# Writing the order of an image's work as one list, with norm sums on VectorE and pruning sums on ScalarE

## The chip, the cores and the metric

The kernel runs on one core of one Trainium2 chip. The metric is the device time of one execution in microseconds (us). Most executions of a kernel agree within 0.3% (41 of the kernel before, taken with e1_psv: 2678.42 to 2688.64 us, median 2684.96). Each ratio below is between fast runs of a kernel and of the kernel before that ran on the same chip in alternation. Where two edited kernels are held against each other, they often ran on different chips; then each goes through its own ratio to the kernel before.

## The reference, cut to what matters

Eight images of 512 channels by 32 x 32, all in fp32. Two residual layers follow each other. Layer 0 is heavy on matmuls, layer 1 on elementwise work.

```python
def reference(x, ...):
    x = x + layer0(group_norm(x))     # 32 groups
    x = x + layer1(group_norm(x))
    return x

def layer0(x):                        # C = 256
    t = silu(bn(conv1x1(x)))          # cv1
    ys = [t[:, :C], t[:, C:]]
    for i in range(2):
        z = silu(bn(conv3x3(ys[-1])))
        z = attention(z)              # 4 heads of 64, 1024 positions; q, k, v from a 1x1 conv
        z = silu(bn(conv1x1(z)))
        ys.append(ys[-1] + z)
    return silu(bn(conv1x1(concat(ys))))    # cv2, the last convolution

def layer1(x):
    h = relu(bn(depthwise3x3(x) + b))
    h = where(max|h| of the channel < 4.0, 0, h)      # pruning
    h = relu(bn(conv1x1(h) + b))
    return where(max|h| of the channel < 1e-3, 0, h)  # pruning
```

## The kernel before

TensorE (PE) does the matmuls of one image after another, and layer 1 of image b-1 is done beside layer 0 of image b: its depthwise taps run on VectorE (DVE), while PE is in the convolutions and attention of the next image. Each engine is given its instructions in the order in which the program emits them. A helper makes sure that no scheduler changes that:

```python
class InOrder:                 # every engine but GpSimd is wrapped in it
    ...
    if self.last is not None:
        self.tc.add_manual_dep(made.ins, self.last, how, reason="in_order")
```

So the text of the program is the queue of each engine. Background work lies in lists of pieces, and the main flow takes a few off a list here and there with `pump(list, n)`. The parts that the argument needs:

```python
def reaches(t, i):             # pruning test: a pass on ScalarE and a 0.15 us test on VectorE
    keep = small.tile([P, 1], F32, tag="keep3", name="keep3")
    nc.scalar.activation(
        work_tile("over"), t, AF.Relu, bias=below[:, i : i + 1], accum_out=keep
    )
    nc.vector.tensor_scalar(keep, keep, 0.0, None, ALU.is_gt)
    return keep
...
    def prune(c):              # layer 1, after the depthwise taps of chunk c
        if c < 2:
            keep = reaches(ht[c], 0)
        else:
            keep = small.tile([P, 1], F32, tag="keep", name="keep")
            nc.vector.tensor_reduce(keep, ht[c], AX.X, ALU.max)
            nc.vector.tensor_scalar(keep, keep, 4.0, None, ALU.is_ge)
        nc.gpsimd.tensor_scalar(ht[c], ht[c], keep, 1.0, ALU.mult, ALU.mult)
    ...
    for c in range(KC):
        mine = [lambda c=c, t=t: tap(c, t) for t in range(9) if t != 4]
        if c:                  # two taps of a chunk carry the end of the chunk before
            mine[2] = lambda c=c, t=mine[2]: (t(), relu(c - 1))
            mine[5] = lambda c=c, t=mine[5]: (t(), prune(c - 1))
        taps += mine
    taps += [lambda: relu(KC - 1), lambda: prune(KC - 1)]
...
def qkv(l, bg, counts):
    ...
    pump(bg, counts.pop(0))
    for m, ps in enumerate(products((2, 3), b == 0)):      # PE: ps_qk, two banks
        ...                                                # VectorE empties a bank into kr
        nc.vector.tensor_tensor(kk, phases(flat(ps)), col..., ALU.add)
        nc.gpsimd.tensor_tensor(kk, kk, row..., ALU.add)
        pump(bg, counts.pop(0))
    for g in range(2):
        ps = ps_big.tile([P, 4, C2], F32, tag="big", name="ps_v")   # needs one of the two banks
        ...                                                # PE: ps_v
        nc.scalar.copy(vt[:, 4 * g : 4 * g + 4, :], ps)
        pump(bg, counts.pop(0))
    for m in range(2):
        (ps,) = products((m,))
        nc.scalar.copy(qy[:, m, :], flat(ps))
        pump(bg, counts.pop(0))
...
    qkv(0, taps, (3, 0, 3, 2, 2, 2, 0))                    # images 1 to 7
```

In the first attention a softmax denominator is used in `scale` (`if s in (29, 30): scale(0, s - 29)`). In the last convolution the pieces of the next image's group norm (`pump(stats)`) stand between products. Layer 1 takes its norm sums with two ScalarE passes per chunk.

## Time and profile before

| | |
|---|---|
| time | 2683.93 us median of 3 runs (2683.41 to 2686.81) |
| PE | 2605.2 us busy; its steady steps sum to 2538 us |
| VectorE, ScalarE | 1999.7 us, 1252.0 us busy |
| lateness of PE by image 0 ... 7 | 30.5, 5.4, 12.1, 12.1, 12.1, 12.1, 14.9, 30.3 us |

"Lateness" is what PE's matmuls start later than the steady step of their kind would have them start, summed over an image; the prediction gives the steps. A name such as ps_v stands for the matmuls that write the tile of that name: ps_qk and ps_v make an attention's queries, keys and values, ps_s its scores, ps_av the sums of values weighted with them, ps_dn the sums of the softmax denominators; pm and pv are the two small ones of a group norm (means, then deviations, from the VectorE tiles mv and d), and ps_pw is layer 1's 1x1 convolution. Read the busy shares and slices first to find the engine that sets the end, then who that engine waits for, then the timeline around the longest wait. The prediction shows these. Two more lines carry the argument here. The chain of work that ended last, by engine:

```profile
PE 76%; DVE 16%; ACT 4%; issue 2%; DMA 1%; POOL 0%; SPq 0%; ACTq 0%; POOLq 0%; DVEq 0%
```

And VectorE's pruning test in the view of groups (count, busy us, mean ns, then the idle time ahead of it and what ended it):

```profile
L43 DVE TENSOR_SCALAR keep<-keep 128x1 f32<-128x1 f32 x64 | 9.8, 153 | 37.9 <-ACT over L43 36.4
```

64 instructions of 0.15 us, and VectorE stood 37.9 us in front of them. VectorE is not the engine that sets the end, so this may cost nothing; it costs something where PE needs VectorE next.

### The profile page before, as it was taken

The numbers are of one execution on the slowest core, as the hardware profiler recorded it, in microseconds if no ns is written. First come the engines' busy times: TensorE is split into PE (matmuls) and PEld (weight loads), VectorE is DVE, ScalarE is ACT, GpSimd is POOL, SyncE is SP. The second block draws the span as 40 slices with busy tenths as digits, with TensorE's granted clock in tenths as the row PEclk, the third lists the DMA queues.
The fourth block names the chain that finished last, engine by engine and source line by source line (L and its number), as shares of the span: only waits on it lengthen the run. The fifth ranks groups of instructions, "written<-read, shape, count | busy, mean of one in ns | idle before, by whom it ended". The sixth has DMA issues, their size and how long they took to land.

```text
span 2685.7 us, 36237 instructions
## 1 busy us (share of the span) xinstructions
PE 2605.2 (97%) x14862; PEld 1364.0 (51%) x14862; DVE 1999.7 (74%) x2708; ACT 1252.0 (47%) x1609; POOL 162.7 (6%) x99
## 2 busy tenths in 40 slices
PE   7999999999999999999999999999999999999996
PEld 5364464644636446364554545455464544645442
DVE  8786588776886768867788677886777866788556
ACT  3535545255453554535544345544445344453544
POOL 1000010000100001000010000100001000010000
PEclk9999999999999999999999999999999999999998
DMA  8443231411304013040231312222131221303100
GB/s 331 153 149 124 66 135 32 145 31 65 137 25 153 16 63 138 24 153 17 79 121 40 138 32 96 89 71 107 32 133 52 83 95 51 118 16 98 56 16 33
DMA packets 74238, 235.99 MB, mean 88 GB/s; under 512 B 6096, under 2 KB 34000, under 8 KB 59984
## 3 DMA queue, kind: packets, MB, share of 16 engines
q1 hardware_dynamic: 70512, 230.19, 24.4%
q10 hardware_dynamic: 3552, 3.41, 0.4%
q8 instruction: 118, 1.93, 0.3%
q14 instruction: 56, 0.46, 0.1%
HBM read 183.77 MB, written 33.03 MB: 81 GB/s over the span
## 4 chain that ended last, share of the span: by engine, by line
PE 76%; DVE 16%; ACT 4%; issue 2%; DMA 1%; POOL 0%; SPq 0%; ACTq 0%; POOLq 0%; DVEq 0%
PE ps_s L43 13%; PE ps_av L43 13%; PE ps_cv L43 9%; PE ps_pw L43 7%; PE ps_c L43 7%; PE ps_cv2q L43 7%; PE ps_qk L43 6%; PE ps_v L43 4%; DVE sum L43 4%; PE ps_m L43 4%; PE ps_y L43 3%; DVE mid L43 2%; DVE ht L43 2%; DVE y L43 1%; PE ps_dn L43 1%
## 5 line engine op out<-in xcount | busy, mean ns | idle before, releaser
L43 ACT ACTIVATE e<-ps_s 128x1024 f32<-128x1024 f32 x512 | 522.6, 1023 | 273.7 <-PE ps_s L43 263.9
L43 PE MATMUL ps_s<-qy,kr 64*64 64x512 f32 x4096 | 583.6, 593 | 3.8 <-ACT e L43 1.6
L43 PE MATMUL ps_av<-e,vt 64*64 64x512 f32 x4096 | 584.0, 591 | 1.6 <-ACT part L43 1.6
L43 DVE TENSOR_TENSOR sum<-sum,e 128x1024 f32<-128x1024 f32 x384 | 470.1, 1224 | 69.8 <-ACT e L43 62.4
L43 DVE SCALAR_TENSOR_TENSOR ht<-xn,v_sb,ht 128x961 f32<-128x961 f32 (+1 forms) x256 | 340.7, 1334 | 10.2 <-ACT ht L43 6.0
L43 PEld LDWEIGHTS ps_av<-e,vt 64*64 64x64 f32 x4096 | 206.1, 133 | 254.2 <-issue 198.3
L43 PEld LDWEIGHTS ps_s<-qy,kr 64*64 64x64 f32 x4096 | 191.1, 133 | 270.6 <-issue 164.8
L43 PE MATMUL ps_pw<-ht,wpw_sb 128*128 128x512 f32 x512 | 229.5, 604 | 7.6 <-DVE wpw_sb L43 7.6
L43 PE MATMUL ps_qk<-z,wring 128*128 128x512 f32 x512 | 228.9, 598 | 3.6 <-ACT z L43 3.6
L43 DVE TENSOR_TENSOR sum<-e 128x1024 f32<-128x1024 f32 x64 | 78.3, 1223 | 186.8 <-ACT e L43 186.2
L43 PEld LDWEIGHTS ps_pw<-ht,wpw_sb 128*128 128x128 f32 x512 | 97.4, 193 | 131.4 <-issue 121.4
L43 PEld LDWEIGHTS ps_qk<-z,wring 128*128 128x128 f32 x512 | 97.0, 191 | 122.5 <-issue 108.9
L43 PE MATMUL ps_v<-wring,z 128*128 128x256 f32 x512 | 118.3, 391 | 19.6 <-DVE kr L43 19.6
L43 ACT COPY c<-ps_c 128x256 f32<-128x256 f32 x96 | 35.4, 369 | 210.3 <-PE ps_c L43 204.1
L43 DVE RECIPROCAL r<-ps_dn 128x128 f32<-128x128 f32 x128 | 114.8, 928 | 11.8 <-ACT r L43 11.8
L43 PEld LDWEIGHTS ps_c<-kr,wring 128*128 128x128 f32 x1024 | 116.9, 192 | 10.3 <-issue 6.2
L43 PEld LDWEIGHTS ps_v<-wring,z 128*128 128x128 f32 x512 | 99.7, 196 | 43.7 <-DVE kr L43 26.2
L43 PE MATMUL ps_c<-kr,wring 128*128 128x128 f32 x1024 | 117.3, 275 | 2.2 <-ACT kr L43 2.2
L43 PE MATMUL ps_c<-vt,wring 128*128 128x128 f32 x1024 | 117.2, 275 | 0.7 <-ACT c L43 0.7
L43 PE MATMUL ps_c<-qy,wring 128*128 128x128 f32 x1024 | 117.6, 276 | 0.2 <-issue 0.2
L43 PE MATMUL ps_cv<-pt,w_sb 128*128 128x512 f32 x256 | 117.4, 609 | 0.0
L43 PEld LDWEIGHTS ps_c<-qy,wring 128*128 128x128 f32 x1024 | 116.1, 192 | 0.4 <-issue 0.3
(176 smaller groups left out, 3169.1 us busy)
## 6 DMA issues: line engine op xcount, KB each, us to landing
wring<-u SPq DMA_DIRECT2D x96, 1024.0 KB, 4.8
pt<-in_x SPq DMA_DIRECT2D x32, 512.0 KB, 6.5
rw<-r SPq DMA_DIRECT2D x64, 256.0 KB, 3.3
xt<-in_x SPq DMA_DIRECT2D x32, 512.0 KB, 5.9
out<-xt SPq DMA_DIRECT2D x32, 512.0 KB, 2.9
wring<-in_wqkv SPq DMA_DIRECT2D x16, 768.0 KB, 4.2
wring<-s SPq DMA_DIRECT2D x12, 1024.0 KB, 5.6
wring<-s SPq DMA_DIRECT2D x12, 768.0 KB, 5.2
```

The source lines that it names most:

```text
L43: made = method(*args, **kwargs)
```

## The change

The intent is to fix the order of all engines' queues in one written list per image. All work is cut into named pieces; a word takes the next piece of that name, `t*2` takes two. What was glued together (a tap with a relu, a pruning pass with its test, a matmul of the norm with what follows it) becomes separate words. A middle image has 449 words for 527 pieces and a closing list of 101 words. Two kinds of sum change engine as well: layer 1's norm sums go from ScalarE passes to VectorE's bn_stats, and all of layer 1's input pruning goes to ScalarE passes.

```diff
+HEAD = """
+    c*2 b im id bm c ca iv t ip t l t*2 lr ib b c bm ca b t y t*2 d y bm d ya d ya d*5 y P Rc ya
+    R d*2 P Rc R d P d Rc R B P Rc R B P B Rc R E P Rc B Ez R E Ez y k*3 ya X k ka dp kp t lp ka
+    t*2 kp t*2 v*2 va t l t v*2 va t*2 lr lp q*4 qa s qa s e*2 t p s t e w t p s e w p l s*2 w
     ... (ten more lines; and FIRST, TAIL and LAST alike)
-    def pump(bg, n=1):
+    def go(plan, without=()):
+        for word in plan.split():
+            name, _, n = word.partition("*")
+            if name in without:
+                continue
+            for _ in range(int(n or 1)):
+                todo[name].pop(0)()
...
-    def reaches(t, i):
+    def excess(t, i):
         keep = small.tile([P, 1], F32, tag="keep3", name="keep3")
         nc.scalar.activation(
             work_tile("over"), t, AF.Relu, bias=below[:, i : i + 1], accum_out=keep
         )
+        return keep
+
+    def positive(keep):
         nc.vector.tensor_scalar(keep, keep, 0.0, None, ALU.is_gt)
-        return keep
...
-        gn = [group_norm_scalar(xt, normed, chunks) for chunks in groups]
+        for chunks in groups:
+            group_norm("i im id iv ip ib b", xt, normed, chunks)
...
+        def reach(c):
+            keep[c] = excess(ht[c], 0)
+
         def prune(c):
-            if c < 2:
-                keep = reaches(ht[c], 0)
             ... (and the VectorE reduction for chunks 2 and 3)
+            positive(keep[c])
...
+            add("t", *[lambda c=c, t=t: tap(c, t) for t in range(9) if t != 4])
+            add("l", lambda c=c: relu(c))
+            add("lr", lambda c=c: reach(c))
+            add("lp", lambda c=c: prune(c))
```

The words used below: `k` a ps_qk product, `ka` its emptying into kr by VectorE, `kp` GpSimd's part of it, `v` and `va` a ps_v product and its copy, `t` a tap, `l` a relu, `lr` a pruning pass on ScalarE, `lp` its test on VectorE, `X` the load of ScalarE's exponential table (1.28 us in image 6 of the changed kernel, from the end of one activation at 1975.92 to 0.01 us before the next), `e` an exponential, `w` its addition to the sums, `h` the scaling of a half of the values, `nc` a check of the denominators, `x0` a residual half and `i` a half chunk's norm sums.

## The prediction

> **What bounds the kernel now.** I read the page's busy shares first, then the slices, then who waited for whom on PE, then the timeline around the longest of those waits.
>
> ```profile
> span 2685.7 us, 36237 instructions
> PE 2605.2 (97%) x14862; PEld 1364.0 (51%) x14862; DVE 1999.7 (74%) x2708; ACT 1252.0 (47%) x1609; POOL 162.7 (6%) x99
> PE   7999999999999999999999999999999999999996
> PEclk9999999999999999999999999999999999999998
> ```
>
> PE is busy in every slice but the first and last, so PE sets the end and only PE's lost time can be won. Busy time hides part of that loss, because the drawn ends of matmuls overlap the next start. So I work from start times in the timeline: at full clock, records of 512 columns start 0.4295 us apart, of 256 columns 0.2155, of 128 columns 0.1117, and four 64x64 records [...] share one step of 0.4295. With the counts of the groups view: 2720 x 0.4295 + 512 x 0.2155 + 3072 x 0.1117 + 8192/4 x 0.4295 + 256/4 x 0.4295 + about 10 for the small ones of the norms = 1168 + 110 + 343 + 880 + 27 + 10 = 2538 us. The change leaves all of these matmuls. The span has 2686 - 2538 = 148 us more: 7.8 before PE's first record, 10.2 after its last start, some 129 between. Adding up the late starts by image (each begins with its first ps_cv record) gives about 30 us for image 0, 5 for image 1, 12 for each of 2 to 5, 15 for 6 and 30 for 7.
>
> PE's waits, from the waits view of PE alone:
>
> ```profile
> PE ps_v L43 <- DVE kr L43: 19.6, 8, 3.1
> PE pv L43 <- DVE d L43: 8.7, 8, 1.2
> PE ps_dn L43 <- DVE sum L43: 8.2, 6, 1.4
> PE pm L43 <- DVE mv L43: 7.8, 1, 7.8
> PE ps_pw L43 <- DVE wpw_sb L43: 7.6, 3, 3.7
> PE pm L43 <- ACT ht L43: 4.3, 2, 2.3
> ```
>
> Columns: who waited for whom, us in total, times, longest. Nearly all is PE waiting for a late VectorE. Measured by start times the same places cost an image of the middle 3.25 us (ps_v), 2.0 (ps_dn) and 1.33 (pv); the rest of its 12 us is many steps of 0.1 to 0.5 us. Image 1 has neither of the first two, and shows what a good order reaches: 5.4.
>
> The timeline of image 6 at the ps_v wait:
>
> ```profile
> 2019.13 0.15 DVE L43 TENSOR_SCALAR keep<-keep 128x1 f32<-128x1 f32 x1 [3.47 <-ACT over L43]
> 2019.20 3.23 DVE L43 SCALAR_TENSOR_TENSOR ht<-xn,v_sb,ht 128x992 f32<-128x992 f32 x2
> ...
> 2022.36 3.82 DVE L43 TENSOR_TENSOR kr<-ps_qk,v_sb 128x1024 f32<-128x1024 f32 x2
> 2024.35 5.92 PE L43 MATMUL ps_v<-wring,z 128*128 128x256 f32 x13 [3.08 <-DVE kr L43]
> ```
>
> VectorE stood 3.47 us before a 0.15 us pruning test that waits for ScalarE, then did depthwise taps, and only then emptied the ps_qk bank that ps_v needs. Nothing here is short of throughput; the order is wrong.
>
> [...] the taps stood ready behind that test for 3.47 us. So the written order is the order done. [...]
>
> ```profile
> 2008.00:2020.60 12.60, 12.60 (x48) 6.85 (x47) 7.46 (x17) 6.02 (x8) 1.15 (x1) 1.00 0.88 336
> 2020.60:2023.30 2.70, 0.67 (x2) 0.00 (x0) 2.70 (x2) 0.83 (x1) 0.82 (x1) 1.00 0.01 6
> 2023.30:2030.10 6.80, 5.75 (x14) 4.59 (x15) 6.76 (x4) 0.41 (x1) 4.80 (x2) 0.50 0.00 0
> ```
>
> Columns: window, length, busy us (records) of PE, PEld, DVE, ACT, POOL, then the granted clock. It is 0.50 after the gap; PE starts there are 2.9 us later than the steady step. The late starts inside such half-clock stretches sum to about 17 us in the kernel, some 14 of them after waits in its course. [...]
>
> **The change part by part.** Rows for the sizes (groups, one row per shape):
>
> ```profile
> L43 ACT ACTIVATE ht<-xt 128x1024 f32<-128x1024 f32 x32 | 33.5, 1048 | 15.4 <-DVE xt L43 15.4
> L43 ACT ACTIVATE ht<-xt,gm 128x1024 f32<-128x1024 f32 x32 | 36.4, 1139 | 20.4 <-DVE gm L43 20.4
> L43 DVE BATCH_NORM_STATS2 st<-pt 128x6 f32<-128x512 f32 x64 | 40.9, 681 | 4.7 <-DMA pt<-in_x 4.7
> L43 DVE TENSOR_REDUCE keep<-ht 128x1 f32<-128x1024 f32 x14 | 17.0, 1212 | 0.0
> L43 ACT ACTIVATE over<-ht,below 128x1024 f32<-128x1024 f32 x18 | 20.5, 1141 | 0.1
> ```
>
> 1. Norm sums of layer 1 to VectorE. The built programs show 64 ScalarE passes gone (33.5 + 36.4 and 2 x 6.0 for their accumulator reads = 82 us) and 64 bn_stats (0.681), 32 aggregates (0.209) and 54 small operations (0.16) more on VectorE: 43.6 + 6.7 + 8.6 = 59 us.
> 2. The layer-1 input pruning to ScalarE: 14 reductions gone (17.0 us of VectorE), 14 passes with read (1.141 + 0.188) more: 18.6 us on ScalarE. Sum: VectorE 2000 + 42 = 2042 us, ScalarE 1252 - 63 = 1189. Neither is the bound, so this alone moves no time; what counts is where it falls. The added sums lie in the closing stage of an image (last convolution), the removed ones in the first attention, where VectorE is fullest.
> 3. The order. Matmul counts stay the same. For a middle image I walked the lists with the durations above:
>  - ps_v: the first bank is now emptied after the second of four ps_qk pieces (1.72 us each) with no tap ahead; 1.98 us end within the 3.44 of the two pieces left. The second follows one tap and ends some 2 us into the 3.44 us of the first ps_v group. The 3.25 us go; so do the half-clock stretches after it (2.9 in image 6, 1.6 in image 7).
>  - ps_dn: three value pieces (0.86 each) stand between the last exponential and the sums. The exponential and its addition (1.02 + 1.22) fit into 2.58. The 2.0 go.
>  - pv: a whole product (3.44 us) now stands between the two norm matmuls, for 0.65 us of VectorE. The 1.33 go.
>  - Two taps move from the first part to the closing stage; with two reductions less, VectorE has 2 x 1.33 + 2 x 1.21 = 5.1 us less up to the end of the first attention: about 109 us (its durations less 5%, as starts overlap) for PE's 126.
>  - Closing stage: VectorE has about 43 us for PE's 56, in spite of the sums.
> So images 2 to 6 fall to about 4.3 us of lateness: 4 x 7.7 + 10.5 = 41; image 1 gives 1. Image 7 has the first part too: 3.25 + 2.0 + 1.6 = 7, and its norm chain at the end, where PE waited 4.3 us for ScalarE's passes, perhaps 2 more; its end stays bound by taps. Image 0's start is bound by the weight transforms on VectorE in both; I give 5. Sum: 41 + 1 + 9 + 5 = 56. I add back 1 for small new waits: 2684 - 55 = **2629**; the written lists look searched for image 0 and the end too, for which I take another 4: **2625 us**.
>
> **The rivals.**
> - *VectorE becomes the bound in the first part.* Between the last product of an image and the first transformed convolution it has about 19 us of taps, norm and residual work, then 5.4 of input transform, against 24.1 us of PE; one late tap stalls PE. For it: VectorE is busy 85% in 670 to 737 us already. Against: drawn durations exceed its real steps by about 0.08 us. At 2 us an image: 2640.
> - *A new wait takes the old one's place.* PE is in order too, and norm matmuls now wait for VectorE where ScalarE served; all pruning passes also take a work buffer. If half of the gain returns: 2655.
> - *The lists remove nearly all lateness, also in images 0 and 7.* With 4 us in each middle image, 18 in the outer two, and shorter throttled stretches: 2610.
>
> **Range and chances.** Eight times in ten between 2608 and 2648; the low end is the third rival, the high end the first plus a part of the second. A gain over 2% needs less than 2630: 0.60. Within 2%: 0.39. Slower by over 2%: 0.01, as PE's work does not change and slack is large.
>
> **What would show it.** Right: PE's wait of ps_v for kr falls from 19.6 to under 3 us, ps_dn for sum and pv for d nearly vanish, no half clock in mid-kernel, VectorE about 2040 us busy, ScalarE about 1190, images of some 320 us instead of 327.5. Wrong: PE waiting for convolution inputs (ps_c for kr), for z or for e, or images 0 and 7 changing by more than 15 us. One thing I saw in the built order: in images 1 to 6 the sums of a chunk are read before its last residual half is added; that would change values a little, not the time.

## The result, and the profile after

| | before | after |
|---|---|---|
| time, median (range) of 4 runs each | 2684.28 us (2683.41 to 2686.81) | 2624.26 us (2622.55 to 2626.34) |
| PE, VectorE, ScalarE busy | 2605.2, 1999.7, 1252.0 | 2578.2, 2020.8, 1179.0 |
| lateness by image 0 ... 7 | 30.5, 5.4, 12.1 x 4, 14.9, 30.3 | 24.5, 4.0, 4.3, 4.0, 4.0, 4.0, 4.0, 14.9 |
| its sum | 129 | 64 |

The ratio is 0.9775 (95% interval 0.9758 to 0.9792): faster by 2.25%. Ratios here are the mean time of one kernel's fast runs over that of the other's of the same rounds, so they are not quite the ratio of the medians.

The page of the changed kernel, to be held against the lines at the head of the prediction:

```profile
span 2621.1 us, 36162 instructions
PE 2578.2 (98%) x14862; PEld 1328.7 (51%) x14862; DVE 2020.8 (77%) x2844; ACT 1179.0 (45%) x1509; POOL 169.9 (6%) x99
```

PE has the same 14862 matmuls, and they take 27 us less "busy" time. Some 10 us of that, at most, is half clock (the clock is at 0.50 for 31 us before and for 10 after); where the rest comes from was not looked for. Who PE waited for, of the changed kernel (us in total, times, longest):

```profile
PE pm L105 <- DVE mv L105: 9.5, 2, 7.8
PE ps_pw L105 <- DVE wpw_sb L105: 5.4, 2, 4.7
PE pv L105 <- DVE d L105: 4.2, 5, 0.8
...
PE ps_v L105 <- DVE kr L105: 1.1, 2, 0.8
```

ps_v for kr fell from 19.6 to 1.1 us, ps_dn for sum from 8.2 to nothing that is listed. What is left at the head of the list stands in image 0 and image 7. The chain of work that ended last, by engine:

```profile
PE 90%; DVE 4%; ACT 3%; issue 1%; DMA 0%; POOL 0%; SPq 0%; POOLq 0%; DVEq 0%; ACTq 0%
```

And the pruning test in the view of groups:

```profile
L105 DVE TENSOR_SCALAR keep<-keep 128x1 f32<-128x1 f32 x64 | 9.6, 150 | 11.0 <-ACT over L105 10.0
```

VectorE's share of the chain went from 16% to 4%, and its standing in front of the 64 tests from 37.9 to 11.0 us. The timeline of image 6 at the place where the prediction showed the ps_v wait (weight loads left out):

```profile
1974.55 7.03 PE L105 MATMUL ps_qk<-z,wring 128*128 128x512 f32 x16
...
1978.18 1.98 DVE L105 TENSOR_TENSOR kr<-ps_qk,v_sb 128x1024 f32<-128x1024 f32 x1 [4.21 <-PE ps_qk L105]
...
1981.20 0.14 DVE L105 TENSOR_SCALAR keep<-keep 128x1 f32<-128x1 f32 x1
1981.41 5.78 PE L105 MATMUL ps_v<-wring,z 128*128 128x256 f32 x26
```

VectorE now stands idle for 4.21 us, waiting for PE, and PE goes from ps_qk to ps_v without a gap. The test comes without a wait: its pass ran on ScalarE long before. Two things are different from before at this place, then: no taps ahead of kr, and no wait at the test. Which of the two matters is what the experiments had to find.

### The profile page after: what moved, and what is told of

Its sections match the earlier page's. It is cut to its first block, busy times and chain, and to the rows that moved or that the text cites. A ratio compares the mean times of both kernels' runs of the same rounds, so it can differ in the third digit from the quotient of the medians.

```text
span 2621.1 us, 36162 instructions
## 1 busy us (share of the span) xinstructions
PE 2578.2 (98%) x14862; PEld 1328.7 (51%) x14862; DVE 2020.8 (77%) x2844; ACT 1179.0 (45%) x1509; POOL 169.9 (6%) x99
## 4 chain that ended last, share of the span: by engine, by line
PE 90%; DVE 4%; ACT 3%; issue 1%; DMA 0%; POOL 0%; SPq 0%; POOLq 0%; DVEq 0%; ACTq 0%
PE ps_av L105 16%; PE ps_s L105 15%; PE ps_c L105 12%; PE ps_cv L105 10%; PE ps_qk L105 8%; PE ps_cv2q L105 8%; PE ps_pw L105 8%; PE ps_v L105 4%; PE ps_m L105 4%; PE ps_y L105 4%; PE ps_dn L105 1%; DVE ht L105 1%; ACT qy L105 1%; ACT e L105 0%; ACT over L105 0%
## 5 line engine op out<-in xcount | busy, mean ns | idle before, releaser
L105 ACT ACTIVATE e<-ps_s 128x1024 f32<-128x1024 f32 x512 | 510.6, 1023 | 272.7 <-PE ps_s L105 262.2
L105 PE MATMUL ps_s<-qy,kr 64*64 64x512 f32 x4096 | 537.9, 592 | 4.4 <-ACT e L105 3.1
L105 PE MATMUL ps_av<-e,vt 64*64 64x512 f32 x4096 | 536.3, 590 | 1.4 <-ACT part L105 0.7
L105 DVE SCALAR_TENSOR_TENSOR ht<-xn,v_sb,ht 128x961 f32<-128x961 f32 (+1 forms) x256 | 326.7, 1283 | 8.5 <-ACT ht L105 5.0
L105 PEld LDWEIGHTS ps_av<-e,vt 64*64 64x64 f32 x4096 | 183.9, 133 | 271.2 <-issue 237.5
L105 PEld LDWEIGHTS ps_s<-qy,kr 64*64 64x64 f32 x4096 | 173.6, 132 | 281.5 <-issue 169.8
L824 POOL TENSOR_TENSOR kr<-kr,v_sb 128x1024 f32<-128x1024 f32 x32 | 75.8, 2370 | 993.6 <-DVE kr L105 993.6
L105 PEld LDWEIGHTS ps_c<-vt,wring 128*128 128x128 f32 x1024 | 115.6, 192 | 3.8 <-issue 3.8
```

The costliest lines, as they stand in the source:

```text
L105: made = method(*args, **kwargs)
L824: nc.gpsimd.tensor_tensor(kk, kk, row.to_broadcast(full), ALU.add)
```

## The experiments

Theory at the outset: PE lost its time to the order of the queues, and each of the three waits of a middle image (ps_v 3.25, ps_dn 2.0, pv 1.33 us) goes when the order at its place is mended. Rival 1: the moves of sums between engines bring the gain. Rival 2: an order mended in one place only moves the wait. Every kernel here gave a correct result and every profile was of the fast state.

### One place at a time, in the kernel before

e1_psv, no tap ahead of the emptying of the banks:

```diff
-            qkv(0, taps, (3, 0, 3, 2, 2, 2, 0))
+            qkv(0, taps, (0, 0, 6, 2, 2, 2, 0))
```

> The kernel before with one edit: the three taps (and the pruning test among them) that stand ahead of emptying the ps_qk banks in the first attention block now stand behind it. Theory (only the order of VectorE's queue is at fault): PE's wait of ps_v for kr, 3.25 us in each of images 2 to 7, goes, and with it the half-clock stretches after two of them (4.5 us): 2684 - 24 = about 2660. Rival (VectorE is too full there, so a delayed tap makes something else late): no more than 8 us gained, 2676 or more, with PE waiting instead for sums or exponentials in the first attention.

Measured: 2692.23 us, ratio 1.0027 (1.0020 to 1.0035). A miss. The waits of PE in this kernel no longer have the ps_v wait near the top; another stands there:

```profile
PE ps_qk L43 <- ACT vt L43: 20.1, 6, 3.4
```

The timeline of image 3 (counted from 0) shows how:

```profile
1048.63 1.24 ACT L43 ACTIVATE ht<-ht,bi,sc 128x1024 f32<-128x1024 f32 x1 [10.24 <-DVE ht L43]
...
1050.82 3.70 PE L43 MATMUL ps_qk<-z,wring 128*128 128x512 f32 x8 [3.35 <-ACT vt L43]
```

Six pieces now stand together behind the banks. One is a tap with a relu glued to it. On ScalarE that relu stands ahead of the two copies that free ps_v's banks, and it waits 10.24 us for a tap that VectorE reaches late. PE waits 3.35 us where it had waited 3.1. In this stretch a mended queue of VectorE is paid for in ScalarE's queue. Part of the rest is half clock: it now follows this wait in images 2, 4, 5, 6 and 7, where the kernel before has it in images 6 and 7 only (mean granted clock of the profiled runs 0.993 and 0.994). Image 3, without it, is 327.8 us long against 327.5.

e2_dn moves `scale(0, .)` from steps 29 and 30 of the attention to 32 and 33, so that its two VectorE operations no longer stand ahead of the last sums:

> The kernel before with one edit: the two scalings of z in the attention stand behind the last addition of exponentials instead of ahead of it. Theory (order): the wait of ps_dn for the last addition, 2.0 us in each of images 2 to 7, goes: 2684 - 12 = about 2672. Rival (VectorE too full, or the wait only moves to the next user of z): under 4 us gained, 2680 or more, with PE waiting at ps_m or ps_pw.

Measured: 2686.30 us, ratio 1.0008 (1.0000 to 1.0017). The ps_dn wait went from 8.2 to 3.3 us in the trace, about 0.8 us an image; a 1.21 us pruning reduction still stands among the last sums. A miss, yet most middle images became longer, not shorter (328.4 us for 327.5), though no wait in them grew. What grew is half clock. The windows view of 3.4 us behind the ps_v wait of image 3, which no edit touched, in the kernel before and in e2_dn (columns as in the prediction, the third number from the end is the granted clock):

```profile
1041.80:1045.20 3.40, 3.40 (x16) 3.01 (x17) 3.37 (x3) 0.00 (x0) 3.40 (x2) 1.00 0.02 5
1042.30:1045.70 3.40, 3.40 (x9) 2.75 (x10) 3.37 (x3) 0.00 (x0) 3.40 (x2) 0.53 0.02 5
```

The wait is 3.25 us in both. In e2_dn half clock follows it in each of images 2 to 7, and costs 1.6 us or more a time (0.47 x 3.4 in this window); all its 12 runs have a mean granted clock of 0.991 or 0.992, the kernel before 0.994 to 0.997. So the edit won about 0.8 us an image, and the clock took it back.

e123 takes e1, e2 and one more edit, which puts a product between the two matmuls of the next image's norm:

```diff
-            pump(stats)
             product(0, "s3")
+            pump(stats)
```

> The kernel before with three edits of order: the two of the other runs, and one more product between the two norm matmuls of the closing stage (1.33 us in each of images 1 to 6 lost there). No engine gets other work. Theory (order): the gains add up, 24 + 12 + 8 = 44 us: about 2640, that is some three quarters of what the whole change gave (60). Rival (engine balance is needed too): they do not add up, 2655 or more.

Measured: 2678.25 us, ratio 0.9971 (0.9958 to 0.9983). The pv wait fell from 8.7 to 1.7 us, ps_dn for sum is at 3.3, and ps_qk for vt stays at 20.1. A gain of 7 us, where the three waits sum to over 36; the time is on the rival's side (2655 or more). Here too half clock follows the vt wait in images 2, 4, 5 and 6 (mean granted clock 0.993); image 3, without it, is 325.6 us long, 2.2 less than in e1_psv.

### The engines alone, and the order alone

m12_engines is the kernel before with both moves of sums and its old order:

```diff
-        gn = [group_norm_scalar(xt, normed, chunks) for chunks in groups]
+        gn = [group_norm(xt, normed, chunks) for chunks in groups]
-            if c < 2:
+            if c < KC:
                 keep = reaches(ht[c], 0)
```

> The kernel before, in its old order, with the two moves of work alone: norm sums of layer 1 on VectorE, all pruning sums of layer-1 inputs on ScalarE. Theory (order): the middle images keep their lengths to within 1 us (327.5), as the late waits stay; only the norm chain at the very end gets shorter, by up to 5 us: 2679 to 2684. Rival (balance): VectorE is relieved in the first attention by 2.4 us an image and the waits there shrink: 15 us or more gained, 2669 or less.

Measured: 2683.89 us, ratio 0.9995 (0.9986 to 1.0004). Two of the waits of PE:

```profile
PE pv L43 <- DVE d L43: 11.0, 14, 1.2
PE ps_qk L43 <- ACT z L43: 7.7, 8, 2.1
```

The ps_dn wait is gone from the list, since no reduction stands ahead of the sums, and the ps_v wait is the 19.6 us that it was. These two grew (from 8.7 and 3.6 us), pm and ps_c start somewhat later too, and together they take what ps_dn gave: a middle image has 12.2 us of lateness instead of 12.1.

o12_order is the reverse: the changed kernel's list, with the norm sums as ScalarE passes and the reduction on VectorE for chunks 2 and 3 (the old bodies under the words `i im id iv ip ib b`, `lr` and `lp`).

> The changed kernel's written order and split pieces, but with the old engines: norm sums of layer 1 as ScalarE passes, and the pruning maximum of two chunks as a VectorE reduction (images 0 to 6), each at the place that the list gives to the piece. Theory (the order carries most of the gain, the engines serve the order): VectorE busy some 1980, ScalarE some 1240; ps_v for kr stays gone; 2628 to 2645 us, with some of the 2.0 us a middle image of ps_dn for sum back, since a 1.21 us reduction stands again on VectorE near the sums. Rival (the moves to other engines carry the gain): over 2665 us.

Measured: 2630.91 us (2626.30 to 2638.16), ratio 0.9798 (0.9781 to 0.9814). ScalarE is busy 1235.0 us, VectorE 1986.1. So 53 of the 60 us come with the order alone. A middle image has 4.2 us of lateness, against 4.0 with the new engines; that ps_dn would come back was wrong, the new order has room for the reduction too. What differs lies at the ends: image 7 has 20.4 us against 14.9, and PE's waits list has pv waiting 4.8 us for ScalarE's passes there. By start times pv is 2.3 us later in sum than in the changed kernel; two stretches of half clock, at 2561.9 and 2582.4 (0.76 and 0.74 in the two windows of 3.4 us from 2560.2, 0.77 and 0.73 in those from 2580.6), stand behind these waits and make most of the rest. Image 0 has 33.0 against 24.5 in the profiled runs; its waits for weights from memory differ from profile to profile (among PE's waits ps_c waits 2.8 us for the DMA of wring in o12_order, 1.4 in d1_delay, and is not listed with it in the changed kernel), and these four runs spread over 12 us, so I take nothing from that difference.

### What in the order

If the order brings the gain, one place of it undone must cost its share. d1_delay puts the three taps back ahead of the emptying of the banks:

```diff
-    ... y k*3 ya X k ka dp kp t lp ka t*2 kp t*2 v*2 va ...
+    ... y k*3 ya X t lp t*2 k ka dp kp ka kp t*2 v*2 va ...
```

> The changed kernel with three taps (and their relu) put back ahead of the emptying of the ps_qk banks, nothing else. Theory (the wait of ps_v for kr cost what its length says, plus the half clock that follows it): PE waits again some 2 to 3.3 us at ps_v in each of images 1 to 7, 14 to 23 us in all, half clock returns in some of them; 2640 to 2655 us. Rival (time lost there is won back at a later place, where PE waits less): under 2632 us.

(The edit moves the three taps and the test; no relu moves with them.) Measured: 2624.99 us, ratio 0.9780 (0.9764 to 0.9797). The changed kernel had 0.9775: the taps cost nothing there, and the ps_v wait is still 1.1 us. My reading of that wait was wrong in a part. The timeline of image 6:

```profile
1977.27 3.24 DVE L105 SCALAR_TENSOR_TENSOR ht<-xn,v_sb,ht 128x992 f32<-128x992 f32 x2
...
1980.44 1.97 DVE L105 TENSOR_TENSOR kr<-ps_qk,v_sb 128x1024 f32<-128x1024 f32 x1
...
1983.55 5.78 PE L105 MATMUL ps_v<-wring,z 128*128 128x256 f32 x26
```

PE fills the two banks from 1976.69 on. The test takes its 0.15 us at 1977.15 without a wait, the taps run while PE fills the first bank, and the bank is emptied by 1982.4, before PE asks for it at 1983.55. Taps alone are not late. So the cause should be the other thing at this place in the kernel before: VectorE's 3.47 us at the test, whose ScalarE pass had just been issued and stood behind z, y and a 1.28 us table load.

Two kernels test that, one from each side. Before they ran I made one more mistake. e1c is the kernel before with the counts `(0, 0, 2, 2, 1, 0, 7)`, written to keep relu and pass out of the copies' way:

> The kernel before with the counts of taps around the first qkv changed from 3,0,3,2,2,2,0 to 0,0,2,2,1,0,7: no tap ahead of the emptying of the ps_qk banks (as in e1_psv), and now also no relu or pruning pass of layer 1 ahead of the copies of vt and qy on ScalarE that could wait for a late tap. Theory (the miss of e1_psv was a relu that waited for its tap ahead of the vt copy): ps_v for kr under 3 us, ps_qk for vt under 4 us, and 2655 to 2668 us. Rival (in this kernel's grain any place for these seven taps costs PE about as much, because VectorE has no room for them at all in the first part): a new wait of over 10 us in sum by PE at the start of the first attention (for qy, e or sum), and over 2678 us.

Measured: 2689.10 us, ratio 1.0022 (1.0014 to 1.0031). ps_v has 1.1 us in the list of PE's waits and vt is off it; at its head stands ps_s waiting 19.7 us for exponentials. In the trace a relu and a pruning pass now stand on ScalarE ahead of the first exponentials, and PE starts 2.56 us late in a middle image for those. It is the rival's case, for these counts. Half clock adds to it in all of images 1 to 7 but 4 (mean granted clock 0.992). e1c23m12 adds e2, e3 and m12 to it:

> The kernel before with all five edits: the tap counts of e1c, the scaling three steps later (e2), the product ahead of the second norm piece (e3), norm sums on VectorE and all layer-1 pruning sums on ScalarE (m12). This rebuilds what I hold for the core of the change without its list. Theory: the three waits of the middle images (3.25, 2.0 and 1.33 us) go, 12 us of lateness become about 6: 2638 to 2655 us. Rival (finer interleaving by single instructions is needed, the coarse pieces give each gain back elsewhere): over 2668 us.

Measured: 2672.12 us, ratio 0.9958 (0.9941 to 0.9974). The late exponentials stay, so it misses its numbers and is on the rival's side (over 2668). Against e1c, which ran on the same chip in the same rounds, it is 17.0 us faster, and most middle images go from 12.6 to 9.0 us of lateness. That looks like the worth of ps_dn and pv (2.0 + 1.33), but is not: of images 2 to 6, half clock follows the wait for exponentials in 2, 3, 5 and 6 of e1c, and in 4 alone of e1c23m12 (mean granted clock 0.992 and 0.995). With half clock an image has 328.1 and 326.2 us, without it 326.4 and 324.5. So the edits are worth 1.9 us an image, and the other 1.7 is the clock. By start times ps_dn and pv gave 3.2 us; 2.0 of it came back at ps_qk, pm and ps_c, as in m12_engines, and 0.6 more was won at ps_s.

e4_split is the kernel before with the pruning of a chunk cut in two. The pass stays where it was; the test follows three taps later. The three taps stay ahead of the banks. Two things move along and were not tried apart: one count of taps, so that a relu does not stand ahead of the first vt copy, and the VectorE reduction of chunk 2, which goes to the end of the list.

```diff
                 mine[2] = lambda c=c, t=mine[2]: (t(), relu(c - 1))
-                mine[5] = lambda c=c, t=mine[5]: (t(), prune(c - 1))
+                mine[5] = lambda c=c, t=mine[5]: (t(), reach(c - 1))   # the pass, on ScalarE
+            if c > 1:
+                mine[0] = lambda c=c, t=mine[0]: (t(), prune(c - 2))   # the test, on VectorE
...
-            qkv(0, taps, (3, 0, 3, 2, 2, 2, 0))
+            qkv(0, taps, (3, 0, 2, 2, 3, 2, 0))
```

> The kernel before with the pruning of a chunk on ScalarE cut in two: the pass is issued where it was, its 0.15 us test on VectorE three taps later; and the counts of taps 3,0,2,2,3,2,0 instead of 3,0,3,2,2,2,0, so that a relu does not stand ahead of the first vt copy. The three taps stay ahead of the emptying of the ps_qk banks. After d1_delay I hold that the taps were never the cause. Theory (VectorE's stand of 3.47 us at the test, whose pass waits on ScalarE behind z, y and a table load, is the whole ps_v wait): ps_v for kr from 19.6 to under 4 us with no wait of over 8 us in its place, 2655 to 2668 us. Rival (VectorE has no room in this stretch, the time shows up at vt, qy or e as in e1_psv and e1c): over 2678 us.

Measured: 2654.12 us (2652.60 to 2655.01), ratio 0.9888 (0.9873 to 0.9904). This edit brings 30.5 us, half of the whole change, and a little more than was expected. Image 6:

```profile
2000.42 1.14 ACT L43 ACTIVATE over<-ht,below 128x1024 f32<-128x1024 f32 x1
2000.66 2.02 DVE L43 TENSOR_TENSOR kr<-ps_qk,v_sb 128x1024 f32<-128x1024 f32 x1
...
2003.65 6.64 PE L43 MATMUL ps_v<-wring,z 128*128 128x256 f32 x30
...
2006.88 0.17 DVE L43 TENSOR_SCALAR keep<-keep 128x1 f32<-128x1 f32 x1
```

ScalarE does z, y, table load and pass as before. VectorE does its three taps (from 1996.98) and the bank meanwhile, instead of standing until 2001.6, and comes to the test 5 us after the pass ended. Images 2 to 6 have 7.7 us of lateness each (from 12.1, and 14.9 in image 6), image 7 has 20.2 (from 30.3); images 6 and 7 gain more because the half clock behind the wait goes too. By start times the 4.4 us of image 3 lie where the theory has them: 3.35 at ps_v, 0.6 at ps_s, 0.44 at ps_dn.

d2_stand is the other side: the changed kernel with d1's taps and the pass of that chunk issued directly ahead of its test, behind the table load, instead of some 36 us earlier as d1_delay has it (1940.77 to 1977.15 in image 6; the 25 us of the text below was a guess).

```diff
-    ... t ip t l t*2 lr ib b c bm ca ...
+    ... t ip t l t*2 ib b c bm ca ...
-    ... y k*3 ya X k ka dp kp t lp ka t*2 kp t*2 v*2 va ...
+    ... y k*3 ya X t lr lp t*2 k ka dp kp ka kp t*2 v*2 va ...
```

> The changed kernel with the three taps ahead of the emptying of the banks as in d1_delay (which cost nothing), and now also the pruning pass of that chunk issued directly ahead of its test and behind the table load, as in the kernel before, instead of some 25 us earlier. Theory (the stand at the test is the cause): VectorE stands 2 to 3.5 us before keep, PE waits 2 to 3.3 us at ps_v in images 1 to 7, 2640 to 2655 us. Rival (the stand is absorbed by the new order as the taps were): under 2632 us.

Measured: 2650.14 us (2649.77 to 2651.06), ratio 0.9875 (0.9860 to 0.9890), where d1_delay, on another chip, has 0.9780: 25 to 26 us lost by the place of a single 1.3 us pass. Image 6:

```profile
1997.37 1.13 ACT L105 ACTIVATE over<-ht,below 128x1024 f32<-128x1024 f32 x1
...
1998.63 0.15 DVE L105 TENSOR_SCALAR keep<-keep 128x1 f32<-128x1 f32 x1 [3.48 <-ACT over L105]
...
2001.86 3.81 DVE L105 TENSOR_TENSOR kr<-ps_qk,v_sb 128x1024 f32<-128x1024 f32 x2
...
2003.81 2.55 PE L105 MATMUL ps_v<-wring,z 128*128 128x256 f32 x8 [2.19 <-DVE kr L105]
```

VectorE stands 3.48 us, as it did before the change (3.47), and PE waits 2.19 us. The windows view of the same place (window, length, busy us of PE, PEld, DVE, ACT, POOL, then the granted clock) shows what follows:

```profile
2003.80:2007.20 3.40, 3.39 (x11) 2.79 (x12) 3.36 (x3) 0.00 (x0) 3.36 (x2) 0.69 0.00 0
2007.20:2012.00 4.80, 4.80 (x21) 4.10 (x20) 4.73 (x3) 2.15 (x2) 1.45 (x1) 0.86 0.00 0
```

From the mean clocks of 0.69 and 0.86 over these windows I estimate a stretch at half clock of some 3.4 us (0.31 x 3.4 + 0.14 x 4.8 = 1.7 us lost, and at a clock of 0.50 half of the stretch is lost). Half clock follows the wait in five of the six images from 1 to 6 (in images 2, 3 and 5 the windows of 3.4 us from 710.6, 1033.6 and 1679.6 have 0.63, 0.81 and 0.68). So an image loses 4.15 us there: 2.35 of waiting and about 1.8 of half clock. Image 4 has the wait without the half clock and loses 2.4.

### A version that goes on from the change

The changed kernel still has two waits that are order. In image 0 PE waits 3.10 us for an exponential:

```profile
262.76 0.60 ACT L105 ACTIVATE r<-ps_dn 128x512 f32<-128x512 f32 x1 [4.64 <-DVE r L105]
...
264.42 1.09 PE L105 MATMUL ps_s<-qy,kr 64*64 64x512 f32 x8 [3.10 <-ACT e L105]
```

A check of the denominators stands on ScalarE ahead of the exponential and waits for the fourth reciprocal, which VectorE begins at 261.79; the exponential begins at 263.35. In the middle images layer 1's relu, pass and another check stand on ScalarE ahead of a copy of attention values, which costs PE 0.7 us.

There is also a defect, seen before the change was run. In the changed kernel's images 1 to 6 the sums of some chunks are read before their last residual half is added. VectorE in image 3 of the changed kernel:

```profile
1265.97 1.28 DVE L105 BATCH_NORM_STATS2 st<-xt 128x6 f32<-128x512 f32 x2
...
1270.64 0.21 DVE L105 BATCH_NORM_AGGREGATE mv<-st 128x2 f32<-128x12 f32 x1
...
1276.68 0.69 DVE L105 TENSOR_TENSOR xt<-c,xt 128x512 f32<-128x512 f32 x1
```

The residual halves come in the order chunk 0, 1, 1, 0. Chunk 0's sums are read at 1265.97, the fourth half is added at 1276.68, after both chunks' sums are closed. Halves are every other pair of columns, so both sums of chunk 0 lack it; chunks 2 and 3 are dealt with in the same way. The output passed the comparison, but the norm is not the one that the reference has.

b1 mends both waits and the defect (chunks taken in reverse in these images, so that a chunk is read after its last half):

```diff
 FIRST: -    ... w nr s p e ns w nc w s e p w h s nc s e p w e p w s e p w z ...
        +    ... w nr s p e ns w w s e p w h s nc s e p w e p w nc s e p w z ...
 HEAD:  -    ... e*2 nc l lr p lp w nc h sc ...
        +    ... e*2 nc l p w h lr lp nc sc ...
 TAIL:  -    ... Q i*2 x0*2 ga Q i u0 a0 i im id Q iv ip u1 x0 Q u1*2 ...
        +    ... Q x0*2 i*2 ga Q u0 a0 x0 i*2 im id Q iv ip u1 Q u1*2 ...   (and the second pair alike)
```

> An attempt at a better version: the changed kernel with the norm sums of a chunk read only after its last residual half (chunks taken in reverse in the quartered images), the check pass of image 0's second softmax put behind three more exponentials, and in the middle images the scaling of the sums put ahead of layer-1 pieces on ScalarE. Theory (the last PE waits are queue order too): 3.3 us in image 0 and 0.7 in each of six images go, 2615 to 2621 us, ratio to the changed kernel 0.997. Rival (the list is already at a local best, each move makes a new wait): 2622 to 2632 us.

Measured: 2628.32 us (2625.95 to 2628.57), ratio 0.9791 (0.9778 to 0.9805), a little slower than the changed kernel. Both waits are gone from the trace. In their place PE waits for the later sums, 1.6 us in each of images 2 to 6: pm waits 17.3 us for mv, where the changed kernel has 9.5. b2 leaves the defect and takes the two edits of FIRST and HEAD alone:

> The changed kernel with the two list edits of b1 alone (the check pass of image 0's softmax behind three more exponentials; in the middle images the scaling of the sums ahead of layer-1 passes on ScalarE), and the norm sums where the change has them. In b1 the trace shows both waits gone, 3.3 us once and 0.7 us an image, against 1.6 us an image of PE waiting for the later norm sums. Theory (the list edits win what their waits were, the sums cost what their wait is): images 1 to 6 at 318.8 us against 319.5 of the changed kernel, image 0 at 312 to 313; 2615 to 2620 us. Rival (b1's miss lay in the list edits): 2622 us or more.

Measured: 2615.53 us (2614.03 to 2617.31), ratio 0.9747 (0.9734 to 0.9761). Images 1 to 6 are 318.6 us long and have 3.1 us of lateness each, image 0 is 311.9 us long. It is the fastest kernel of this study, by 2.5% against before and, through the kernel before, by about 0.3% against the change (0.9747 / 0.9775 = 0.9971; the two intervals just overlap, but the profiles show the same, 318.6 us an image for 319.5). It has the change's defect. Between b1 and b2 only the place of the norm sums and of the pieces next to them differs: 12.8 us between their medians (on two chips; 11.8 by their ratios), 5.0 against 3.1 us of lateness in a middle image. So reading the sums early is worth some 1.8 us an image in this list. A changed kernel with correct sums and nothing else was not run; from these numbers I estimate 2624 + 13 = 2637 us for it, without a new search of its order. That would be 1.8% faster than the kernel before, where the change has 2.25%. b1 is the fastest kernel here whose sums are complete.

| kernel | median us | ratio to before |
|---|---|---|
| e1_psv, e2_dn, e123 | 2692.2, 2686.3, 2678.3 | 1.0027, 1.0008, 0.9971 |
| m12_engines | 2683.9 | 0.9995 |
| e1c, e1c23m12 | 2689.1, 2672.1 | 1.0022, 0.9958 |
| e4_split | 2654.1 | 0.9888 |
| o12_order | 2630.9 | 0.9798 |
| the change | 2624.3 | 0.9775 |
| d1_delay, d2_stand | 2625.0, 2650.1 | 0.9780, 0.9875 |
| b1, b2 | 2628.3, 2615.5 | 0.9791, 0.9747 |

## Why the prediction was right, point by point

**The time and the bound.** 2625 us was predicted, 2624.26 measured. PE's lost time was the whole matter: lateness fell by 65.5 us (129.3 to 63.8) and the span of the profiled runs by 64.6 (the profiled run of the kernel before is some 3 us above its median).

**Part 1 and 2, the engines.** "This alone moves no time" holds in the old order: m12_engines is at 0.9995. In the new order the moves are worth 0.2 us in a middle image and 5.5 us in image 7, where PE waited for ScalarE's passes (o12_order). The prediction had "perhaps 2 more" there. ScalarE came to 1179 for 1189, VectorE to 2021 for 2042. The added and removed instructions have the predicted numbers and sizes; what the sum missed is that other records are drawn shorter in the new order. The 256 taps alone went from 340.7 us (1334 ns each in the mean) to 326.7 (1283 ns), which is 14 of the 21; in e4_split, with every instruction of before, VectorE also fell, from 1999.7 to 1990.5. What makes a tap shorter was not tested, and the time does not hang on it.

**Part 3, ps_v.** The size was right (3.25 us a middle image, and the half clock after it), the mechanism in part wrong. The prediction puts the wait down to the stand at the test and the taps after it together, and the gain to the bank being emptied "with no tap ahead". d1_delay shows that the taps are free. e4_split and d2_stand show, from both sides, that the stand of 3.5 us is the cause: a test on VectorE written directly behind a pass on ScalarE whose queue has a table load in it. What the change does about it is the separate words `lr` and `lp`, with some 40 us between them in image 6 (the pass at 1938.64, the test at 1981.20).

**Part 3, ps_dn and pv.** Both went from the middle images. The start times of image 3 say where its 8.1 us were won, from the kernel before to the changed one: 3.37 to 0.02 at ps_v, 2.94 to 0.53 at ps_dn, 1.40 to nothing at pv, 1.69 to 0.74 at ps_s; ps_av lost half a microsecond (0.99 to 1.53). So the three places of the prediction make 7.3 of the 8.1. For ps_v the cause is shown. For ps_dn and pv the size is read from the traces, but neither was undone singly in the changed kernel, and in the old order their gain was taken back at once: by half clock in e2_dn, by new small waits in m12_engines and e1c23m12. That the list has no such waits is seen; which word of it keeps them away was not tested.

**Images.** Middle images were to fall to "about 4.3" and have 4.0 to 4.3. Image 1 gained 1.4 for 1, image 0 gained 6 for 5. Image 7 gained 15.4 for 9, the largest miss of the sum, and over the 15 us that the prediction itself had named as a sign of being wrong. Its own terms came out: by start times 4.9 at ps_v with its half clock (for 3.25 + 1.6), 2.4 at ps_dn (for 2.0), 2.2 at the norm chain (for 2). What it missed is the very end, for which it has no gain ("its end stays bound by taps"): ps_pw's late starts there fell from 13.2 to 8.3 us, half clock included. The 4 us added for searched lists cover most of this, by luck and not by working. In image 7 three late starts of pv for d, 1.0 us each, remained that the prediction wanted to "nearly vanish".

**Half clock.** None in mid-kernel, as predicted; only two stretches close to the end remain (windows of 3.4 us from 2594.2 and 2614.6 have 0.52 and 0.50). The length of a wait alone did not decide it: the same wait of 3.25 us has none behind it in images 2 to 5 of the kernel before (1.00 in image 3), and has it in all of images 2 to 7 of e2_dn (0.53 in image 3).

**The rivals.** VectorE did not become the bound: in the first part of an image it stands idle 4.21 us before the first bank. "A new wait takes the old one's place" did not come true for the change, but for four of my own smaller edits (e1_psv, m12_engines, e1c and, for the norm sums, b1); in e2_dn it was the clock and no wait. "Nearly all lateness removed", at 2610, is about what b2 then reached.

**What stays open.** Why the waits of image 0 for weights differ between profiles, what decides in which images half clock follows a wait, and whether an order with complete norm sums could reach the time of the change.

## What to carry to other kernels

Where an engine does its work in the written order, as VectorE did here (it stood 3.47 us at a test with two taps written behind it), avoid writing an instruction directly behind the instruction of another engine that it waits for: issue the producer early and put the consumer several pieces later, as separate pieces. That split, with one count of taps moved along, brought half of this gain (30.5 of 60 us), with the same instructions on the same engines. Before moving a piece out of the way, ask what is glued to it and which other queue that will block, since two such moves here (e1_psv, e1c) only carried the wait to another engine's queue. Read the granted clock before judging a small edit: e2_dn shortened its wait and still lost, because half clock fell into more images (granted clock 0.991 or 0.992 in its runs, 0.994 to 0.997 in those of the kernel before). And when a new order reads something earlier than the old one, check that it is complete by then: a part of a gain may be work that is no longer waited for.
